# Moving a group norm's load, statistics and coefficients from attention to the end of the layer before

## The chip, the cores and the metric

The kernel runs on one core of a Trainium2 chip. The metric is the device time of one execution in microseconds (us). Each time below is either that of whole executions, measured without a profile, or comes from the one profiled execution; the text says which.

## The reference, cut to what matters

The input x has 8 batch elements of 512 channels by 32 x 32 positions (1024 positions), all in float32. Two layers run one after the other on each element, and no element needs another one.

```python
# layer 0: group norm, attention with 8 heads, output projection, group norm, residual
hn  = group_norm(x, gn1_scale, gn1_bias)          # 32 groups, statistics over 16 channels x 1024 positions
qkv = einsum('bchw,oc->bohw', hn, w_qkv) + b_qkv  # 8 heads of 64 channels
wgt = softmax(einsum('bct,bcs->bts', q * s, k * s))
a   = einsum('bts,bcs->bct', wgt, v)
x   = x + group_norm(einsum('bchw,oc->bohw', a, w_proj) + b_proj, gn2_scale, gn2_bias)

# layer 1: normalised weights, one head over 512 channels, residual
qkv = einsum('oc,bcn->bon', w_qkv1, x);  qkv = qkv / rms(qkv)
attn = softmax(einsum('bci,bcj->bij', q, k) * 512 ** -0.5)
h   = einsum('oc,bcn->bon', w_out, einsum('bij,bcj->bci', attn, v))
x   = (x + h) * 2 ** -0.5
```

## The kernel before

The kernel works through the elements b = 0 to 7 in a Python loop that is fully unrolled (line 1012). Nearly every instruction goes through `InOrder` (line 26), which pins each engine's instructions to the order in which the program names them. So the text of the program is the schedule: each engine (TensorE is PE, VectorE is DVE or `VE`, ScalarE is ACT or `AC`, GpSimd is POOL or `PO`) works through its own list in order, and SyncE's queue (SP, `SY`) issues the transfers in order. Since every instruction passes through that helper, the profile puts nearly all of them on one line, L34; tiles tell them apart.

**Attention (layer 0).** For each element there are 32 steps (`STEPS`), four pairs of heads by eight blocks of 128 rows. `Heads.step(i, fill, early, later)` (line 490) does this in order: `softmax(i)` (two maxima on DVE, two exponentials on ACT, tiles `nm` and `p`); in odd steps from 5 on `values` (16 calls of a matmul, tile `po`, input `pT`); the `fill` list, which holds TensorE work; `scores(i + 1)` (tile `s`, two score tiles of 128 x 1024); `turn()`, which transposes the probabilities of the step before on DVE (tile `pb`) and sends them to `pT` with four transfers; the `early` list; `scale()` (reciprocal on DVE, two multiplies on POOL); and the `later` list. In even steps the `fill` list holds a part of `project_rows` (tile `pqk`), the query and key projection of the next pair of heads; in odd steps it is empty but for what is said of layer 1 below.

Score tiles come from `ps_s`, which has three buffers, and every `scores` takes two of them. Tiles `po`, `pqk`, `pm` and `pv` come from `ps_m` (`bank`), which has two buffers. Large tiles in SBUF come from seven slots (`Slots`, line 37), which are taken and given back by name in program order.

**Norm 1.** `Norm1` (line 300) belongs to the group norm ahead of attention. It loads nothing itself: `load_x` (line 150) brings a quarter of an element (512 KB) into the tile `hn`. `stats` is one `bn_stats` on DVE for half a quarter, eight in all; `aggregate` is four `bn_aggr` (tile `mv`). `GroupNorm.all_steps` (line 291) then averages over each group with a tiny matmul (tile `pm`, which reads `mv`), computes the variance's input with four small DVE operations (tile `d`), does a second tiny matmul (tile `pv`, which reads `d`), and computes the coefficients with seventeen small DVE operations. `apply` multiplies and adds a quarter in place on POOL. Element b + 1 is treated within the attention of element b: the loads stand in steps 4 to 7, the statistics in steps 6 to 13, the aggregate and the pm matmul in step 14, the rest of the coefficients in steps 15 to 21, and the four multiplies in steps 21 and 22.

**Layer 1.** `Layer1.project` (line 724 on) ends with matmuls into the tiles `e`, the unnormalised weights of the second attention, and gives back the slot of the tile `u`, which those matmuls read. What is left is eight products, for two halves `th` of the positions and four quarters `c` of the channels. Here a product is named po(th, c):

```python
def products(self, th, c):     # 8 matmuls 128x512 into a bank, tile po
def keep(self, th, c):         # DVE: multiply po by 1/sum, then add to the residual x
```

`total(th)` is one matmul (tile `pe`) and a DVE reciprocal of the sums, of 128 x 512 elements. `keep` with `th` = 1 also issues the store of its quarter.

The first four products follow one another. The other four are handed on as `fills` and `laters` to steps 0 to 3 of the next element's attention: step c does po(1, c) ahead of `scores(c + 1)`, and keep(1, c) at its end. After step 3 the slots of the element before are given back (`done`).

Of the kernel before, what the change touches and what calls it, by code (L numbers as in the profile page):

```python
# [52 lines left out]
def attention_blocks_kernel(  # L53
# [26 lines left out]
    B, C, H, W = x.shape  # L80
    N = H * W
    NH, D, GROUPS = 8, C // 8, 32
    CI, NT, HN = C // P, N // P, N // 2
# [20 lines left out]
    PE, VE, AC, PO, SY = (InOrder(tc, e) for e in (nc.tensor, nc.vector, nc.scalar, nc.gpsimd, nc.sync))  # L104

    def big(name, lead=CI):

        return slots.take([P, lead, CI * N // lead], name)
# [14 lines left out]
    def run(pieces):  # L123
        for _ in pieces:
            pass
# [4 lines left out]
    x0 = big("hn_0")  # L130
# [19 lines left out]
    def load_x(b, xt, ci):  # L150
        SY.dma_start(out=xt[:, ci, :], in_=xv[b, :, ci, :])
# [82 lines left out]
    def fetch(name, b):  # L234
        SY.dma_start(out=place(name, b), in_=far[name])
# [102 lines left out]
    def project_qk(b, j, hn):  # L338

        qk = pair.tile([P, 2, N], F32, tag="qk", name=f"qk_{b}_{j}")  # L340
        kp = qk[:, 1, :].rearrange("p (be m) -> p be m", be=4)

        def pieces():
            for t in (1, 0):
                w = near["qk"][:, t]
                for th in range(2):
                    hs = slice(th * HN, (th + 1) * HN)
                    pm = bank(f"pqk_{b}_{j}_{t}_{th}")
                    run(matmuls(pm, [(w[:, ci, j * P : (j + 1) * P], hn[:, ci, hs]) for ci in range(CI)]))
                    if t == 0:  # L350
                        AC.activation(qk[:, 0, hs], pm, AF.Identity, bias=bqs[:, j : j + 1], scale=QSCALE0)
                    else:
                        AC.activation(
                            kp[:, :, th * P : (th + 1) * P],
                            pm.rearrange("p (m be) -> p be m", be=4),
                            AF.Identity,
                            bias=col(BK, j),
                        )
                    yield

        return qk, pieces()

    def project_rows(b, j, hn):

        qk = pair.tile([P, 2, N], F32, tag="qk", name=f"qk_{b}_{j}")
        kp = qk[:, 1, :].rearrange("p (be m) -> p be m", be=4)
        spare = near["v#"]

        def pieces():
            for t in (1, 0):
                w = near["qk"][:, t]
                scale = 1.0 if t else QSCALE0
                bias = col(BK, j) if t else bqs[:, j : j + 1]
                for th in range(2):
                    hs = slice(th * HN, (th + 1) * HN)
                    pms = [bank(f"pqk_{b}_{j}_{t}_{th}_{r}") for r in range(2)]
                    for ci in range(CI):
                        for r in range(2):  # L380
                            PE.matmul(
                                pms[r],
                                w[halves[r], ci, j * P : (j + 1) * P],
                                hn[halves[r], ci, hs],
                                start=(ci == 0),
                                stop=(ci == CI - 1),
                            )
                    to, rest = qk[:, 0, hs], spare[:, hs]
                    if t:

                        to = kp[:, :, th * P : (th + 1) * P]
                        rest = rest.rearrange("p (be m) -> p be m", be=4)
                        pms = [pm.rearrange("p (m be) -> p be m", be=4) for pm in pms]
                    AC.activation(to, pms[0], AF.Identity, bias=bias, scale=scale)
                    AC.activation(rest, pms[1], AF.Copy, scale=scale)
                    yield lambda to=to, rest=rest: PO.tensor_add(to, to, rest)

        return qk, pieces()
# [545 lines left out]
    norm1 = Norm1(0, x0)  # L944
# [6 lines left out]
    coeffs = norm1.gn.all_steps()  # L951
# [39 lines left out]
    v0_0 = big("v0_0", NT)  # L991
# [6 lines left out]
    qk0, todo = project_qk(0, 0, x0)  # L998
# [6 lines left out]
        slots.give(name)  # L1005


    heads = Heads(0, x0, v0_0, qk0)
    fills = [[lambda: next(v0)] for _ in range(CI)]
    laters = [[] for _ in range(CI)]  # L1010
    heads.scores(0)
    for b in range(B):
        hn, more = heads.hn, b + 1 < B
        todo = iter(())
        for i in range(STEPS):
            j, r = divmod(i, NB)
            due = []
            fill = [lambda: due.append(next(todo, None))] if (i - LAG) % RG else []
            early, later = [], []
            if i < CI:  # L1020
                fill, later = fills[i] + fill, laters[i]
            if r == 0:
                if j + 1 < CI:
                    heads.qk[j + 1], todo = project_rows(b, j + 1, hn)
                elif more:
                    qk_next, todo = project_rows(b + 1, 0, hn_next)
                if j + 1 == CI:
                    slots.give(f"hn_{b}")
                    if not more:
                        o_last = big(f"o_{b}")  # L1030
                        todo = project_out_half(b, heads, o_last)
            later.append(lambda: [f() for f in due if f])

            if more:


                if i == CI:
                    hn_next = big(f"hn_{b + 1}")
                    norm1 = Norm1(b + 1, hn_next)
                if 0 <= i - CI < CI:  # L1040
                    later.append(lambda: load_x(b + 1, hn_next, i - CI))
                if 0 <= i - CI - 2 < 2 * CI:
                    later.append(lambda: norm1.stats((i - CI - 2) // 2, i % 2))
                k = i - 3 * CI - 2
                if k == 0:
                    coeffs = norm1.gn.all_steps()
                    early += [norm1.aggregate, lambda: next(coeffs)]
                elif 0 < k < 8:
                    early.append(lambda: next(coeffs, None))
                if 0 <= k - 7 < CI // 2:  # L1050
                    for ci in range(2):
                        later.append(lambda ci=ci: norm1.apply(2 * (k - 7) + ci, PO))

            if i == STEPS - NB + 1:
                xt = big(f"x_{b}")
            if 0 <= i - (STEPS - NB + 1) < CI:
                later.append(lambda: load_x(b, xt, i - (STEPS - NB + 1)))
            heads.step(i, fill, early, later)

        if more:  # L1060
            v0_next = big(f"v0_{b + 1}", NT)
            v0 = project_v0(b + 1, hn_next, v0_next)
            next(v0)
        heads.values(STEPS // RG - 2)
        heads.turn()
        if more:
            fetch("proj7", b)
            ta = big(f"ta_{b}").rearrange("p (k i) (h n) -> p k i h n", k=2, h=2)
            rhs = RightSide(heads.a, ta[:, 0], ta[:, 1])
            for j in range(CI // 2 + 1):  # L1070
                rhs.sums(j)
            for _ in range(3):
                next(v0)
        else:
            fetch("score", b)
            begun = OutBegun(b, heads)
        heads.values(STEPS // RG - 1)
        slots.give(f"v0_{b}")
        if more:
            finish_layer0(b, heads, rhs, xt, v0)  # L1080
        else:
            finish_last(b, heads, xt, o_last, begun)
        fetch("value", b)
        one = Layer1(b, xt)
        one.project()
        for c in range(CI):
            one.products(0, c)
            if c == 0:
                one.total(0)
            one.keep(0, c)  # L1090
            if c == 1:
                one.total(1)
        slots.give(f"e_{b}_0")
        if more:
            heads = Heads(b + 1, hn_next, v0_next, qk_next)
            heads.scores(0)
            fills = [[lambda c=c: one.products(1, c)] for c in range(CI)]
            laters = [[lambda c=c: one.keep(1, c)] for c in range(CI)]

            def done(b=b):  # L1100
                for name in (f"v1_{b}", f"e_{b}_1", f"x_{b}"):
                    slots.give(name)

            laters[CI - 1].append(done)
        else:
            for c in range(CI):
                one.products(1, c)
                one.keep(1, c)
# [33 lines left out]
```

## Time and profile before

| what | value |
|---|---|
| runs of the kernel | 3293.03, 3295.05, 3295.7 us; median 3295.05 |
| profiled execution | 3295.35 us, of which the span from the first to the last instruction is 3293.2 |
| PE, DVE, ACT, POOL busy | 99%, 64%, 33%, 30% of the span |
| one `bn_stats` on `hn` (128 x 512) | 0.67 us, 64 of them |
| reciprocal of a sum in layer 1 (128 x 512) | 3.35 us |
| `apply` of a quarter on POOL | 1.19 us |
| one transfer of a quarter into `hn` | 6.1 us from issue to landing |

The busy share says how much of the span an engine spent in instructions. An engine's row in a list of waits says who released it, how long it waited in total, how often, and the longest time. The chain of waits is followed back from the last instruction to whatever released each step, so a hole in TensorE appears there as another engine's piece. A timeline line has the start, the length, the engine, the operation, the tiles (written tile, arrow, tiles read), the shapes, a count, and in brackets the idle time before it with its releaser.

### The profile page before, as it was taken

To read this page: it belongs to the slowest core of one execution; us is meant where nothing else is said; L and a number is where in the kernel's file an instruction comes from. 1 tells how busy PE (TensorE), PEld (TensorE's weight loads), DVE (VectorE), ACT (ScalarE), POOL (GpSimd) and SP (SyncE) were. 2 spreads that over 40 slices of the span, in tenths; PEclk is the share of its full clock that TensorE was granted. 3 is DMA by queue.
4 is the path that set the end of the run, shared out by engine and by line. 5 is a ranking of instruction groups with operands and counts; after the bars stand their busy time and mean duration, and the time that the engine had idled before them with its cause. 6 is when DMAs were issued, how large, how long until landed. Compare 5 with 4: busy or idle time off the path is not lost.

```text
span 3293.2 us, 35605 instructions
## 1 busy us (share of the span) xinstructions
PE 3263.8 (99%) x13178; PEld 1606.6 (49%) x13178; DVE 2118.5 (64%) x2869; ACT 1071.5 (33%) x1813; POOL 983.4 (30%) x857
## 2 busy tenths in 40 slices
PE   8999999999999999999999999999999999999899
PEld 4444544545444454444544445444554545444354
DVE  4696647955488554885449754596645966468653
ACT  2453124521145211551215412254123531145210
POOL 0352123511245022460214503254122531235121
PEclk9999999999999999999999999999999999999899
DMA  5675206741078411782118811287204762057500
GB/s 189 195 196 166 81 6 179 202 150 67 8 205 212 128 45 35 209 219 91 45 53 216 233 52 44 81 219 208 77 13 125 207 177 90 13 140 196 183 7 26
DMA packets 182707, 410.82 MB, mean 125 GB/s; under 512 B 27620, under 2 KB 27656, under 8 KB 176520
## 3 DMA queue, kind: packets, MB, share of 16 engines
q1 hardware_dynamic: 182416, 408.53, 43.6%
q8 instruction: 105, 1.72, 0.2%
q14 instruction: 66, 0.54, 0.0%
q10 hardware_dynamic: 120, 0.02, 0.0%
HBM read 112.48 MB, written 27.56 MB: 43 GB/s over the span
## 4 chain that ended last, share of the span: by engine, by line
PE 94%; DVE 2%; DMA 2%; SPq 1%; issue 1%; DVEq 0%; ACTq 0%
PE po L34 26%; PE s L34 13%; PE pqk L34 12%; PE pv L34 7%; PE p_e_T L34 7%; PE p_e_B L34 5%; PE py L34 4%; PE p_u_T L34 3%; PE p_v_T L34 3%; PE p_o_T L34 3%; PE p_v_B L34 3%; PE p_u_B L34 3%; PE p_o_B L34 2%; DMA pT<-pb 1%; DVE pb L34 1%; PE pG L34 1%
## 5 line engine op out<-in xcount | busy, mean ns | idle before, releaser
L34 POOL TENSOR_SCALAR p<-p,tt 128x1024 f32<-128x1024 f32 x512 | 566.8, 1120 | 917.0 <-DVE tt L34 915.3
L34 ACT ACTIVATE p<-s,nm 128x1024 f32<-128x1024 f32 x512 | 565.9, 1110 | 839.6 <-DVE nm L34 801.1
L34 DVE TENSOR_REDUCE nm<-s 128x1 f32<-128x1024 f32 x512 | 602.1, 1217 | 180.1 <-PE s L34 179.2
L34 DVE STREAM_TRANSPOSE pb<-p 128x2048 f32<-128x2048 f32 x256 | 589.5, 2303 | 29.6 <-POOL p L34 18.8
L34 PE MATMUL s<-qk 64*128 64x512 f32 x2048 | 508.7, 602 | 0.0
L34 PE MATMUL po<-pT,v 128*64 128x256 f32 x4096 | 471.8, 383 | 3.8 <-DMA pT<-pb 2.8
L34 PE MATMUL pqk<-hn,qk 64*128 64x512 f32 (+1 forms) x2016 | 473.9, 591 | 0.0
L34 PE MATMUL po<-e,v 128*128 128x512 f32 x1024 | 450.9, 595 | 0.0
L34 PEld LDWEIGHTS po<-pT,v 128*64 128x64 f32 x4096 | 287.2, 137 | 217.1 <-ACT v L34 68.2
L34 PEld LDWEIGHTS pqk<-hn,qk 64*128 64x128 f32 (+1 forms) x2016 | 201.8, 187 | 252.1 <-issue 240.2
L34 PEld LDWEIGHTS po<-e,v 128*128 128x128 f32 x1024 | 192.2, 190 | 252.7 <-issue 245.5
L34 PEld LDWEIGHTS s<-qk 64*128 64x128 f32 x2048 | 194.4, 186 | 238.8 <-issue 234.2
L34 POOL TENSOR_TENSOR u<-u,xy 128x512 f32<-128x512 f32 x64 | 78.9, 1270 | 762.8 <-DMA xy<-far_rinv 390.2
L34 PE MATMUL pv<-v,hn 128*128 128x512 f32 x512 | 229.0, 598 | 0.0
L34 DVE TENSOR_TENSOR e<-e,p_e_T 128x512 f32<-128x512 f32 x160 | 107.0, 685 | 145.0 <-PE p_e_T L34 142.8
L34 POOL TENSOR_TENSOR qk<-qk,v 128x512 f32<-128x512 f32 x124 | 158.6, 1279 | 83.9 <-ACT v L34 83.9
L34 ACT ACTIVATE e<-e,shift,rinv 128x512 f32<-128x512 f32 x128 | 100.8, 811 | 247.7 <-DVE e L34 247.7
L34 POOL TENSOR_TENSOR esum<-esum,e 128x512 f32<-128x512 f32 x96 | 121.5, 1267 | 163.9 <-ACT e L34 161.4
L34 PEld LDWEIGHTS pv<-v,hn 128*128 128x128 f32 x512 | 94.6, 190 | 115.1 <-issue 114.8
L34 PE MATMUL p_e_T<-s,t 128*128 128x512 f32 x320 | 147.8, 592 | 0.0
L34 PE MATMUL py<-x,gram 128*128 128x512 f32 x320 | 141.6, 602 | 6.0 <-issue 6.0
L34 DVE TENSOR_TENSOR v<-po,esum 128x512 f32<-128x512 f32 x56 | 38.7, 691 | 160.0 <-PE po L34 159.8
(186 smaller groups left out, 3062.3 us busy)
## 6 DMA issues: line engine op xcount, KB each, us to landing
pT<-pb SPq DMA_DIRECT2D x1024, 256.0 KB, 4.4
hn<-in_x_dram SPq DMA_DIRECT2D x32, 512.0 KB, 6.1
x<-in_x_dram SPq DMA_DIRECT2D x32, 512.0 KB, 6.1
out_dram<-x SPq DMA_DIRECT2D x32, 512.0 KB, 3.3
score<-far_score SPq DMA_DIRECT2D x8, 1792.0 KB, 7.6
value<-far_value SPq DMA_DIRECT2D x8, 1792.0 KB, 7.0
qk<-far_qk SPq DMA_DIRECT2D x7, 2048.0 KB, 8.0
proj<-far_proj SPq DMA_DIRECT2D x7, 1792.0 KB, 9.1
```

Of the source, the lines that this page charges most:

```text
L34: return lambda *args, **kw: self._pin(call(*args, **kw))
```

## The change

The norm of element b + 2 is begun at the end of layer 1 of element b. Its tile `hn` is taken there and its four loads are issued ahead of the first product. Six statistics stand behind keep(0, 1) and keep(0, 2), and the last two behind keep(0, 3). The aggregate and the pm matmul come next. Product po(1, 0) and its keep follow outside attention, then the pv matmul and the coefficients, and only then the first scores of the next attention. The other three products stand in steps 0 to 2 of attention, and step 3 has none. The four multiplies stand in steps 1, 3, 5 and 7 of the next element's attention. Element 1 is still treated within the attention of element 0, as before, since nothing comes ahead of it; elements 2 to 7 are treated in the new place.

```diff
@@ steps of attention
-            if more:
+            if b and more and i % 2 and i < 2 * CI:
+                later.append(lambda: norm1.apply(i // 2, PO))
+            if not b:
                 if i == CI:
                     hn_next = big(f"hn_{b + 1}")
                     norm1 = Norm1(b + 1, hn_next)
...
@@ end of layer 1
         one = Layer1(b, xt)
         one.project()
+        hn_now = hn_next
+        if b + 2 < B:
+            hn_next = big(f"hn_{b + 2}")
+            norm1 = Norm1(b + 2, hn_next)
+            for c in range(CI):
+                load_x(b + 2, hn_next, c)
         for c in range(CI):
             one.products(0, c)
             if c == 0:
                 one.total(0)
             one.keep(0, c)
             if c == 1:
                 one.total(1)
+            if c and b + 2 < B:
+                for ci in (0, 1) if c == 1 else (c,):
+                    for k in range(2):
+                        norm1.stats(ci, k)
         slots.give(f"e_{b}_0")
         if more:
-            heads = Heads(b + 1, hn_next, v0_next, qk_next)
+            if b + 2 < B:
+                norm1.aggregate()
+                coeffs = norm1.gn.all_steps()
+                next(coeffs)
+                next(coeffs)
+            one.products(1, 0)
+            one.keep(1, 0)
+            if b + 2 < B:
+                run(coeffs)
+            heads = Heads(b + 1, hn_now, v0_next, qk_next)
             heads.scores(0)
-            fills = [[lambda c=c: one.products(1, c)] for c in range(CI)]
-            laters = [[lambda c=c: one.keep(1, c)] for c in range(CI)]
+            fills = [[lambda c=c: one.products(1, c)] for c in range(1, CI)] + [[]]
+            laters = [[lambda c=c: one.keep(1, c)] for c in range(1, CI)] + [[]]
...
-            laters[CI - 1].append(done)
+            laters[CI - 2].append(done)
```

## Prediction

> **What bounds the kernel now.** I read the page first, then TensorE's own waits, then the chain of waits around the passage from one element to the next, then the timeline of the same stretch. In the page's busy line TensorE (PE) is at 99%, every other engine at 64% or less:
>
> ```profile
> PE 3263.8 (99%) x13178; PEld 1606.6 (49%) x13178; DVE 2118.5 (64%) x2869; ACT 1071.5 (33%) x1813; POOL 983.4 (30%) x857
> ```
>
> So only what TensorE waits for, or what it executes, counts. Its waits, from the list of who waited for whom:
>
> ```profile
> PE py L34 <- issue: 6.0, 1, 6.0
> ...
> PE pm L34 <- DVE mv L34: 4.0, 1, 4.0
> PE po L34 <- DMA pT<-pb: 2.8, 1, 2.8
> ```
>
> Each of these three happened once, all in the last element, which computes no norm1. The attention that holds norm1 today shows no waiting: the windows view gives 42.69 us of busy PE in 42.69 us for 1338.72 to 1381.41, eight steps with statistics in them, 10.67 us a pair of steps, the pace of a pair without them (1403.49 to 1414.16 in the chain). At 64% VectorE (DVE) is not the bound, and freeing it gives TensorE nothing there.
>
> The chain of waits over one passage (element 2 to 3) gives the order that the change alters:
>
> ```profile
> 1269.83 13.73 PE po L34 x32
> 1283.57 1.92 PE s L34 x8
> 1285.48 7.06 PE po L34 x16
> 1292.55 4.05 PE pqk L34 x15
> ...
> 1319.27 1.72 PE s L34 x7
> 1320.99 7.06 PE po L34 x16
> 1328.05 1.92 PE s L34 x8
> 1329.97 3.43 PE pqk L34 x16
> ```
>
> po x16 is one `products` call, s x8 one `scores`. See that a product stands between every two score groups up to step 3, and that PE has no hole. A score group costs 1.92 after a product and 1.72 after pqk; a product 7.06 after scores and 6.87 (half of 13.73) after a product. Each change of shape thus costs 0.2.
>
> What step 3's product hides is in the timeline: scores 3 end at 1320.99, but the first exponential, which frees a score tile, ends at 1322.61:
>
> ```profile
> 1320.18 2.36 DVE L34 TENSOR_REDUCE nm<-s 128x1 f32<-128x1024 f32 x2 [3.94 <-PE s L34]
> ...
> 1321.50 1.11 ACT L34 ACTIVATE p<-s,nm 128x1024 f32<-128x1024 f32 x1 [1.60 <-DVE nm L34]
> ```
>
> The last element shows the chain that the change puts behind `keep(0, 3)`, with TensorE idle in front of it:
>
> ```profile
> 3103.57 1.29 DVE L34 BATCH_NORM_STATS2 st<-o 128x6 f32<-128x512 f32 x2
> 3104.89 0.21 DVE L34 BATCH_NORM_AGGREGATE mv<-st 128x2 f32<-128x12 f32 x1
> 3105.15 0.51 PE L34 MATMUL pm<-mv,gavg 128*128 128x4 f32 x2 [3.95 <-DVE mv L34]
> ```
>
> And the windows view shows what a 2.83 us hole (3075.46 to 3078.29) did to the clock (last columns: granted clock, DMA share, GB/s):
>
> ```profile
> 3078.00:3084.00 6.00, 5.71 (x34) 3.55 (x35) 2.31 (x1) 0.47 (x1) 0.81 (x1) 0.72 0.85 212
> ```
>
> **What the Trainium skill says.** "TensorE: Matmul & The Clock Gate", Part 1, says that TensorE falls to half clock after an idle window of about 3.4 us and needs a busy window of that length to recover; the window runs freely. This trace agrees on the price and is harsher on the threshold: after 2.83 us the 32 po matmuls took 5.18 instead of 3.67, and the clock of 0.72 over 6 us is 3.4 us at half speed, so 1.7 us lost. The same page, Part 3 ("What overlaps and what doesn't"), says that matmuls start and end in program order; the pm above, waiting with everything behind it, agrees. "PSUM — Partial Sum Buffer", Engine vs sequencer instructions, says that VectorE's queue is strict FIFO; the timeline shows nothing else.
>
> **The change part by part.** In the built program PE's order is po(0,3), pm, po(1,0), pv, scores 0; DVE's is keep(0,3), two statistics, four aggregates, four small operations for the mean, keep(1,0), seventeen small operations, first maximum.
>
> *1. A new wait at pm, 6 passages (b = 0 to 5).* pm needs the aggregate, which stands behind keep(0,3), which needs po(0,3) whole. The DVE chain from the end of po(0,3): keep 1.45 (1283.57 to 1285.02: two of 0.69 with gaps), two statistics 1.31, four aggregates 0.38 (attention's row of four), hand-over 0.04: 3.2 us of idle TensorE. Queued behind pm: po(1,0), scores 0, everything. pm itself 0.15 (its pair is 0.32 in today's chain, shape change included; ends 0.05 and 0.5). 6 x 3.35 = +20.1. pv follows po(1,0) by which time d is long ready: 6 x 0.15 = +0.9.
>
> *2. The clock after it.* 3.2 us is longer than the hole that cost 1.7. As the window runs freely I take 70% of six: +7.1; ends 0 and 18.6 (3.1 each, what py lost after the last element's long hole: 20.30 against 17.17).
>
> *3. Step 3 loses its product, 7 passages (b = 0 to 6).* po(1,0) leaves step 0, the others move up one step, step 3's list is empty. Scores 4 follow scores 3 at once, with three score tiles of which they need two: the first is free, the second is the one that exponential 3 frees 1.62 after scores 3. Scores 4 then need two more passes of 0.43, so they end 2.55 after scores 3 instead of 1.72: +0.85. Behind it DVE (maximum, transpose 2.30, maximum) and ACT run late: exponential 4 ends when pqk ends (+0.1), and the drain of pqk, behind exponential 4's second half, holds the bank that values(0) needs (+0.5). By step 6 they have caught up, since a step asks 4.8 us of DVE (2.35 + 2.30 + 0.13) against 5.34 of PE. 7 x 1.45 = +10.2; ends 0.8 and 3.0 each (a whole maximum and exponential, plus a late bank).
>
> *4. Shape changes.* Scores 4 after scores 3 save 0.20, po(1,0) after a 128-row matmul 0.19: 7 x 0.39 = -2.7.
>
> *5. pm and pv leave attention, 6 elements.* In today's chain the pair of steps with pm lasts 11.10 (1381.41 to 1392.51), that with pv 10.98, against 10.67: 6 x (0.43 + 0.31) = -4.4.
>
> *6. Priced at nothing.* Eight statistics (0.67) and the small operations leave attention: no PE wait there today. Six of the statistics run in the 3.0 us hole after the second reciprocal (1270.35, 3.35 long) and in the 5.5 us hole before keep(0,3); four of them end at about 1276.3, keep(0,2) is due at 1276.74. If that cover goes, keep(0,3)'s chain lengthens. The seventeen operations (3.35, timeline of the last element, 3107.13 to 3110.46) put the first maximum 4.8 us after po(1,0); po(1,1) and pqk, 11 us, hide it, and keep(1,1)'s multiply, next on DVE, has 0.4 to spare before pqk wants its bank. Four loads on SP move from steps 4 to 7 to the release of u at 1254.4: SP has only stores behind them, the DMA share there is 0.00, a 2048 KB fetch lands in 8.0, issue takes up to 1.8 each, so all are in by about 1267; DVE asks at 1273.7. On POOL four multiplies of 1.19 move to steps 1, 3, 5, 7, each ahead of the next `scale`, where POOL idles 3 us and more. Slots: hn takes u's place; the pT tiles of steps 1 to 5 get slots whose last readers end about 10 us before or earlier.
>
> **Sum:** 20.1 + 0.9 + 7.1 + 10.2 - 2.7 - 4.4 = +31.2. The profiled execution took 3295.35 (span 3293.2 and 2.15 around it), 0.3 above the median of the runs: 3326.
>
> **Rivals.**
> *A: the clock holds.* The hole stays under the gate's window, pm costs 3.35 only: 3295 + 24 = 3319. For: 3.2 is under the skill's 3.4. Against: 2.83 sufficed once. 14%.
> *B: step 3 runs DVE into arrears.* Transposes then also wait for the pT transfers, of which 1 MB leaves per step (one waited 0.69 at 1343.72): 3.5 us a passage instead of 1.45: 3340. 11%.
> *C, not slower: no hole at pm.* If the statistics of the last quarter and the aggregate were done before po(0,3) ends, pm would find its operand ready. Place: DVE's queue in those 6.87 us, idle for 4 of them. Price: -20.1 - 7.1. It decides from the point where the last statistics stand ahead of keep(0,3). Then 3299, within no change; if exponential 3 is hidden too, 3289. The built order, keep first, speaks against it. 4%.
> *D: the loads come late,* DVE stands in front of keep(0,2) and pm waits 3 us longer: 3345 or more. Seven us of margin say no. 3%.
>
> **How the numbers follow.** The likeliest case, 68%, gives 3326. The range 3309 to 3343 holds A and B, and the ends of 2 and 3 except where both lie at an end together; C and most of D are left out. A measurement tells about 0.2% (6.6 us) from no change: faster 0.02 and same 0.03 are C with and without the exponential, and 0.01 for an error in the sum; slower 0.95.
>
> **What would show it.** TensorE's waits after: "pm from DVE mv" six more times, near 3.2 each; a clock below 1.00 in the windows behind some of them; score groups 3 and 4 adjacent with a hole near 1.2 and a values group half a us late; no pm or pv inside attention from element 1 on. Wrong, if pm's wait is absent or under 2 us, if holes over 3 us appear in step 3, or if DVE waits for hn.

## The result, and the profile after

The changed kernel takes 3330.64 us (median of 6 runs, 3326.19 to 3342.92) against 3295.7 us (median of 6, 3293.03 to 3298.18): a ratio of 1.0111, 95% interval 1.0092 to 1.0131. It is slower by about 1.1%, at 3330.64 against the predicted 3326. Its runs scatter over 17 us, those of before over 5. The profiled execution of the changed kernel took 3334.11 (span 3332.2, which is 39.0 more than before).

TensorE's share fell to 98% while its instruction count stayed the same:

```profile
PE 3272.9 (98%) x13178; PEld 1607.6 (48%) x13178; DVE 2127.5 (64%) x2869; ACT 1073.0 (32%) x1813; POOL 982.7 (29%) x857
```

Who TensorE waited for (total us, times, longest):

```profile
PE pm L34 <- DVE mv L34: 22.1, 7, 4.0
PE s L34 <- ACT p L34: 12.4, 7, 1.8
PE py L34 <- issue: 6.0, 1, 6.0
...
PE po L34 <- DMA pT<-pb: 2.9, 1, 2.9
```

Two rows differ from before. The pm row had one entry of 4.0, in the last element; it now has seven, so the six new ones are 18.1 us, 3.0 each. The wait of the scores for an exponential did not exist; it comes seven times, once per passage (the stretch from one element's layer 1 to the next one's attention), 1.8 each.

The chain of waits over the passage from element 2 to 3 shows both places, each time as pieces of other engines between pieces of PE:

```profile
1285.38 13.75 PE po L34 x32
1299.13 0.02 issue
1299.15 0.70 DVE v L34
1299.85 0.02 issue
1299.88 0.69 DVE x L34
1300.57 1.20 DVE st L34 x2
1301.76 0.34 DVE mv L34 x4
1302.10 0.04 issue
1302.14 0.59 PE pm L34 x2
1302.73 9.64 PE po L34 x16
1312.37 0.12 PE pv L34 x2
1312.49 1.92 PE s L34 x8
...
1348.19 0.89 PE s L34 x5
1349.09 0.02 issue
1349.11 1.24 DVE nm L34
1350.34 0.02 issue
1350.37 0.02 ACTq L34
1350.38 0.04 issue
1350.43 1.21 ACT p L34 x2
1351.64 0.04 issue
1351.68 1.55 PE s L34 x5
```

The upper part is keep(0, 3) (v, then x), the last two statistics (st), the four aggregates (mv), then pm: 3.03 us without TensorE. Then po(1, 0), an ordinary product of 6.87, takes 9.64. The lower part is step 3: maximum 3, exponential 3, and only then scores 4.

What happened to po(1, 0) is in the windows view of this passage and the next one, in which the hole was as long (columns: window, length, five engines, granted clock, DMA share, GB/s):

```profile
1302.70:1312.40 9.70, 9.70 (x19) 4.21 (x18) 0.65 (x4) 0.00 (x0) 0.00 (x0) 0.73 0.00 0
1708.80:1715.80 7.00, 7.00 (x19) 3.17 (x18) 0.64 (x4) 0.00 (x0) 0.00 (x0) 1.00 0.00 0
```

The clock was 0.73 in one and 1.00 in the other. PE is busy throughout in both, so the busy share hides this loss.

I measure a passage from the start of po(0, 0) to the start of the first `values`, both read off the chain. From element 2 to 3 these are, before and after:

```profile
1254.38 6.87 PE po L34 x16
1335.12 3.60 PE po L34 x32
```

```profile
1269.93 6.87 PE po L34 x16
1358.82 3.60 PE po L34 x32
```

Before, a passage is 80.74 us, and the same wherever the chain shows it whole. After, the seven are 88.91, 88.90, 88.89, 86.02, 86.01, 87.71 and 82.38: longer by 8.17, 8.16, 8.15, 5.28, 5.27, 6.97 and 1.64, in sum 43.6. The last one has no norm, and shows step 3 alone: 1.64. Two have norm and full clock: 5.27, of which 3.6 are the hole, pm and pv. The other four lost 2.9, 2.9, 2.9 and 1.7 more, which is the clock, 10.4 in all. Attention between the passages (from the first `values` to the next po(0, 0)) was 318.04 to 318.69 in the six elements 1 to 6 and is 317.31 to 317.39: a gain of 5.7. With 0.8 and 0.2 us lost at the start and in the last element, the sum is 43.6 - 5.7 + 1.0 = 38.9 of the 39.0.

### The profile page after: what moved, and what is told of

It reads as the page before. It is cut to its first block, busy times and chain, and to the rows that moved or that the text cites. A ratio compares the mean times of both kernels' runs of the same rounds, so it can differ in the third digit from the quotient of the medians.

```text
span 3332.2 us, 35659 instructions
## 1 busy us (share of the span) xinstructions
PE 3272.9 (98%) x13178; PEld 1607.6 (48%) x13178; DVE 2127.5 (64%) x2869; ACT 1073.0 (32%) x1813; POOL 982.7 (29%) x857
## 3 DMA queue, kind: packets, MB, share of 16 engines
q8 instruction: 105, 1.72, 0.2%
## 4 chain that ended last, share of the span: by engine, by line
PE 98%; DVE 1%; issue 0%; ACT 0%; DMA 0%; SPq 0%; ACTq 0%; DVEq 0%
PE po L34 27%; PE s L34 14%; PE pqk L34 14%; PE pv L34 7%; PE p_e_T L34 7%; PE p_e_B L34 5%; PE py L34 4%; PE p_u_T L34 3%; PE p_v_T L34 3%; PE p_o_T L34 3%; PE p_v_B L34 2%; PE p_u_B L34 2%; PE p_o_B L34 2%; PE pG L34 1%; PE pA L34 0%; PE pB L34 0%
## 5 line engine op out<-in xcount | busy, mean ns | idle before, releaser
L34 PE MATMUL po<-e,v 128*128 128x512 f32 x1024 | 460.2, 605 | 0.0
```

The source lines that it names most:

```text
L34: return lambda *args, **kw: self._pin(call(*args, **kw))
```

## The experiments

**e1_hole_gone: order on VectorE alone.** The loads and all DVE work of the norm stay at the end of layer 1.

```diff
         for c in range(CI):
             one.products(0, c)
...
+            if c == CI - 1 and b + 2 < B:
+                for k in range(2):
+                    norm1.stats(c, k)
+                norm1.aggregate()
             one.keep(0, c)
...
-            if c and b + 2 < B:
+            if 0 < c < CI - 1 and b + 2 < B:
...
-                norm1.aggregate()
                 coeffs = norm1.gn.all_steps()
```

> The last two statistics and the aggregate stand ahead of keep(0,3) on VectorE instead of behind it; everything else is as in the changed kernel. Theory (the time went into the hole at pm, the slower clock after it, and step 3): the six holes of 3.03 us and every loss of clock vanish, pm costs some 0.15 us instead of 0.39, step 3 keeps its 1.8 us wait: 3304 us, 9 above the kernel before. Rival (the moved loads and statistics crowd the end of layer 1, whatever their order): 3325 to 3335 as in the changed kernel, with the lost time at other waits.

Measured: 3307.88 (ratio to before 1.004, interval 1.0025 to 1.0055), 23 us less than the changed kernel, with runs from 3306.53 to 3309.47. The chain of the same passage:

```profile
1273.81 13.75 PE po L34 x32
1287.56 0.02 issue
1287.58 0.70 DVE v L34
1288.28 0.04 issue
1288.33 7.13 PE po L34 x16
```

The hole at pm is gone and po(1, 0) runs at full pace. The rival that the moved work crowds the end of layer 1, whatever its order, falls: the same work in the same place, in another order on one engine, costs 23 us less. The forecast of 3304 missed 4 us, and the list of waits names them, a wait that the hole had covered:

```profile
PE po L34 <- DVE v L34: 4.0, 6, 0.7
```

There are two banks (buffers for the results of matmuls): pm has taken the one that po(0, 2) left, so po(1, 0) needs that of po(0, 3) and waits for the first half of keep(0, 3), 0.7 us, six times.

**e2_hole_half and e3_hole_long: the length of the hole.** In e2 only the statistics move ahead of keep(0, 3). In e3 the changed kernel gets four more statistics in front of the aggregate:

```diff
+                for k in (0, 1, 0, 1):
+                    norm1.stats(CI - 1, k)
                 norm1.aggregate()
```

> Only the last two statistics move ahead of keep(0,3); the aggregate stays behind it. Theory: the hole shrinks from 3.03 to 1.8 us, and with so short a hole the clock stays at 1.00: 3317 us, with runs close together. If the clock is lost after any hole at all: up to 10 us more, 3327. Rival of crowding: no change from the changed kernel.

> Four statistics are added ahead of the aggregate (the last quarter's two, twice over; the result is the same), so that the hole grows from 3.03 to about 5.6 us. Theory: with a hole longer than any window of the gate, every one of the six passages loses the clock, 2.9 us each as in the worst passages of the changed kernel, in every run: 3324 + 15.7 + 17.4 = 3357 us, and the runs scatter less than those of the changed kernel (3326 to 3343). If the loss were a matter of chance for every length, about 3346 with the same scatter.

Measured: e2 3320.27 (3318.28 to 3322.25; ratio 1.0077, interval 1.0062 to 1.0092), e3 3351.57 (3351.07 to 3352.97; ratio 1.0173, interval 1.0156 to 1.019). The hole of e2 is 1.83 us. My expectation that so short a hole leaves the clock alone was wrong: in three passages it does, in the other three it doesn't. Two neighbouring passages of e2, from the chain:

```profile
489.40 0.39 PE pm L34 x2
489.78 8.67 PE po L34 x16
```

```profile
893.23 0.39 PE pm L34 x2
893.62 6.97 PE po L34 x16
```

The product loses 1.70 us or nothing, never a part. In e3, with a hole of 5.4 us instead of the 5.6 expected, every passage loses: po(1, 0) takes 8.39 to 9.61, and pm 0.59 instead of 0.39. That is 2.2 us a passage on average, where I had written 2.9; with the hole 0.2 shorter, it is why e3 came out 5 us under its forecast. As expected, the runs lie within 2 us of one another, where those of the changed kernel lie within 17.

What decides is when the hole begins. The Trainium skill ("TensorE: Matmul & The Clock Gate", Part 1) states a free-running window of 3413 ns. The trace records the granted clock itself, and it agrees. In the changed kernel the clock falls to 0.50 in four passages, at 488.77, 894.96, 1301.15 and 2516.29, which lie 119, 119 and 356 times 3.4133 us apart; it stays there for two windows (6.83) in the first three and for one (3.41) in the fourth. The windows view around the third fall, and around the first one of e2, with the clock as the third figure from the end:

```profile
1297.74:1301.15 3.41, 1.37 (x4) 0.30 (x2) 1.96 (x4) 0.00 (x0) 0.00 (x0) 1.00 0.01 2
1301.15:1307.98 6.83, 5.84 (x9) 2.74 (x10) 1.59 (x10) 0.00 (x0) 0.00 (x0) 0.50 0.00 0
1307.98:1311.39 3.41, 3.41 (x10) 1.50 (x9) 0.00 (x0) 0.00 (x0) 0.00 (x0) 1.00 0.00 0
```

```profile
486.91:490.32 3.41, 1.56 (x6) 0.68 (x5) 2.15 (x9) 0.00 (x0) 0.00 (x0) 1.00 0.00 0
490.32:493.73 3.41, 3.41 (x5) 1.37 (x5) 0.22 (x2) 0.00 (x0) 0.00 (x0) 0.50 0.00 0
493.73:497.14 3.41, 3.41 (x9) 1.47 (x9) 0.00 (x0) 0.00 (x0) 0.00 (x0) 1.00 0.00 0
```

These instants give the boundaries of the windows in each execution. The next table puts the start of each hole (start of pm less the length of the hole) after the last boundary; e5, described below, has the hole of the changed kernel:

| hole | us from the boundary to the start of the hole, and length of po(1,0) there |
|---|---|
| 1.83 us (e2) | 0.66, 0.87, 1.08: 8.67; 1.51, 1.72, 2.15: 6.97 |
| 3.03 us (changed kernel and e5) | 1.08: 9.80; 1.34, 1.37, 1.40: 9.66, 9.65, 9.64; 1.49, 1.78, 1.89, 2.05: 6.97; 2.52, 2.59, 2.86, 3.33: 8.67 |
| 5.4 us (e3) | 1.20, 1.43, 1.54: 8.56, 8.44, 8.39; 2.49, 2.67, 2.72: 9.61, 9.52, 9.50 |

The places sort the losses of all 24 holes without an exception. The loss is half of what is left of the slow stretch when the hole ends: in the third passage of the changed kernel, the stretch runs for 6.83 and the hole covers its first 0.99, which gives 2.9; a hole that is over before the clock falls costs half a window, 1.70. In e3 the loss therefore falls by half a us for each us that the hole begins later, within each group. The traces do not agree with the skill's advice to avoid idle gaps over about 3 us (same page, "Why this matters for your kernels"): 1.83 us is enough where it falls badly. How much idle time in a window it takes stays open. All of the 1.83 us lay in one window when the hole began at 0.66, and cost 1.70; all of it lay in one window as well when it began at 1.51, and cost nothing.

**e4_product_moved: step 3 alone.** The kernel before, with the norm where it was:

```diff
         if more:
+            one.products(1, 0)
+            one.keep(1, 0)
             heads = Heads(b + 1, hn_next, v0_next, qk_next)
             heads.scores(0)
-            fills = [[lambda c=c: one.products(1, c)] for c in range(CI)]
-            laters = [[lambda c=c: one.keep(1, c)] for c in range(CI)]
+            fills = [[lambda c=c: one.products(1, c)] for c in range(1, CI)] + [[]]
+            laters = [[lambda c=c: one.keep(1, c)] for c in range(1, CI)] + [[]]
```

> The kernel before with one part of the change only: po(1,0) stands ahead of scores 0 and step 3 has no product; the group norm stays within attention. Theory: each of seven passages loses 1.64 us net (2.04 of waiting at scores 4 less 0.39 of shape changes): 3295.4 + 11.5 = 3307 us, no hole at pm, clock 1.00. Rival (step 3 costs only since the norm's multiplies and coefficients stand near it): under 3299 us.

Measured: 3306.8 (3306.5 to 3308.45; ratio 1.0037, interval 1.0024 to 1.005), 11.9 above the 3294.86 of the kernel before, measured beside it, for 11.5 expected. Its list of waits has the same row as the changed kernel:

```profile
PE s L34 <- ACT p L34: 12.4, 7, 1.8
```

So step 3 costs this with or without the norm beside it.

**e5_step3_filled: something else in step 3.** The changed kernel, with pqk moved one step:

```diff
-            fill = [lambda: due.append(next(todo, None))] if (i - LAG) % RG else []
+            fill = [lambda: due.append(next(todo, None))] if (i in (0, 3) if b and i < CI else (i - LAG) % RG) else []
```

> The changed kernel with one pqk part moved from step 2 to step 3 in elements 1 to 7; a product cannot stand in step 3, since the seven slots are all taken there (hn of the element after the next holds one, and pT of step 3 needs the one that v1 gives back). Theory: the 3.43 us of pqk cover exponential 3, so the seven waits of 1.8 us at scores 4 vanish (2.04 us a passage), and pqk no longer waits for a bank behind a product in step 2 (some 0.85 us a passage); the hole at pm and its clock stay: 3330.6 - 20 = 3310 us. Rival (the lost time at step 3 is VectorE in arrears, which would only come out elsewhere): above 3320.

Measured: 3310.44 (3307.05 to 3311.99; ratio 1.0042, interval 1.0026 to 1.0057), the 3310 that was expected. No wait of the scores is left, and the holes at pm stay as they were (22.1 us in seven waits). The last passage, which has no norm, falls from 82.38 to 79.50: 2.04 are the wait at scores 4, and 0.84 are what pqk no longer loses behind a product in step 2. Step 3's loss was a missing cover, not VectorE in arrears.

**e6_both_mended and e7_two_ahead: the terms together.** e6 has the edits of e1 and e5, and pm and pv of this norm in a score tile (`norm1.gn.bank` replaces `bank` there). e7 adds:

```diff
             if b + 2 < B:
                 run(coeffs)
+            one.products(1, 1)
+            one.keep(1, 1)
...
-            fills = [[lambda c=c: one.products(1, c)] for c in range(1, CI)] + [[]]
+            fills = [[], [lambda: one.products(1, 2)], [lambda: one.products(1, 3)], []]
```

> Statistics and aggregate ahead of keep(0,3), as in e1_hole_gone; pm and pv of this norm in a score tile instead of a bank, so that po(1,0) needn't wait 0.66 us for keep(0,3) as it did there; and pqk in step 3, as in e5_step3_filled. Theory: the three terms add, so with all of them gone: 3307.9 - 4.0 - 20.2 = 3284 us, 0.34% below the kernel before, and no wait of TensorE at a passage. If the terms overlap: above 3290.

> As e6_both_mended, and po(1,1) too stands ahead of scores 0, so that step 0 has pqk alone: another 1.24 us for each of seven passages (one change of shape, and pqk's wait for a bank behind a product): 3275 us. If maximum and exponential 0 come late behind the coefficients, up to 2 us a passage are given back: 3285 to 3290.

Measured: e6 3283.02 (ratio 0.9962, interval 0.9949 to 0.9974), e7 3275.1 (ratio 0.9937, interval 0.9925 to 0.995), both within 1 us of the forecast. The terms add up, and both kernels beat the kernel before and the changed one. The chain of e7 at the passage has nothing but PE in it:

```profile
1277.96 0.12 PE pm L34 x2
1278.08 6.97 PE po L34 x16
1285.05 0.12 PE pv L34 x2
1285.17 6.97 PE po L34 x16
1292.14 1.92 PE s L34 x8
1294.06 3.43 PE pqk L34 x16
1297.49 1.72 PE s L34 x8
```

A pm that finds its operand ready costs 0.12. The pqk in step 0, with no product in front of it, takes 3.43 and the scores behind it 1.72, where the two took 6.20 before (1292.55 to 1298.75 in the kernel before): the product ahead of it had cost 1.05 more, a change of shape and a wait for its bank.

**e8_norm_stays: the same products, the old norm.** The kernel before, with po(1, 0) and po(1, 1) ahead of scores 0 and the other two products in steps 1 and 3.

> The kernel before, the norm within attention, but po(1,0) and po(1,1) ahead of scores 0 and the other two products in steps 1 and 3. Theory: 2 x 1.24 us for each of seven passages: 3294.9 - 17.4 = 3277.5 us. Against e7_two_ahead this tells what the moved norm alone is worth once its waits are mended: about 2.5 us, of the 5.7 us that attention gained less what pm and pv cost in the new place. If e7 is not faster than this one, moving the norm brings nothing.

Measured: 3278.47 (3276.96 to 3280.47; ratio 0.9949, interval 0.9937 to 0.9962). Most of e7's gain is thus the place of the products and not the norm. Moving the norm, once nothing waits for it, is worth 3.4 us (3278.47 - 3275.1; the ranges of the runs don't overlap), for 2.5 expected. In the two profiled executions, 3.1 apart, six elements gain 0.74 each in attention (318.05 to 317.31) and lose 0.44 each in the passage (78.25 to 78.69), 1.8 in sum; 0.8 more is one wait at pm in e8.

## Why the prediction was right, point by point

The direction, the size and both places were right. By its steps, with the profiled execution beside them:

1. *The wait at pm:* 20.1 foretold and 0.9 for pv. Measured 6 x (3.03 + 0.39) = 20.5 and 6 x 0.12 = 0.7. The aggregates and statistics were slightly shorter (0.34 and 1.20), pm after a hole longer (0.39 to 0.59). e1 shows the cause.
2. *The clock:* 7.1 foretold, 10.4 measured in this execution. The step took one loss of 1.7 in 70% of passages; three of six lost 2.9, one 1.7, two nothing. The share was about right and the price too low, because the clock can stay down for two windows. Even the hole that the price was taken from lost 1.5 and not 1.7 (5.18 against 3.67): it ended 0.3 after the clock fell. Without its 10.4 this execution would have taken 3323.7. The six runs lie 2.5 to 19.2 above that, 6.9 in the median; this is an estimate of their clock losses, which puts all of their scatter down to the clock. So it is in part luck that 7.1 fits the median run: where a hole falls in the window changes from run to run.
3. *Step 3:* 10.2 foretold (1.45 a passage). Measured 2.04, the net 1.64 and the 0.39 of shape changes together: 14.3 over seven. The mis-sized part is scores 4 in the wait. I let both rows of the first score tile run while the second was awaited; but `scores` alternates between its two tiles, and the trace shows a wait of 1.77 with all but the first of eight passes behind it. The lateness that I placed at the following steps (0.5 for a bank) didn't come: after scores 4 nothing waits. e4 and e5 show the cause.
4. *Shape changes:* -2.7, not measured apart; the 1.64 of the last passage fits it, and e4 with it.
5. *pm and pv out of attention:* -4.4 foretold, -5.7 measured. They account for 0.74 an element, as foretold: e1, with the norm outside, takes 317.30 from values to po(0, 0), and e4, with the norm inside, 318.05. The rest is 0.1 to 0.6 in five elements of the kernel before only, where VectorE's transposes waited for the pT transfers more often (8.4 us in 11 waits, and 3.3 in 7 after):

```profile
2557.26 2.31 DVE L34 STREAM_TRANSPOSE pb<-p 128x2048 f32<-128x2048 f32 x1 [1.37 <-DMA pT<-pb]
```

That line is of the kernel before, in a step that loads hn. Since e4 loads hn in the same steps and shows no such loss, the load alone isn't the cause; this part, 1.3 us in all, stays open.

6. *Priced at nothing:* right. No wait for a transfer into hn appears on VectorE, and the four issues took 1.76 us from 1270.07, right behind the release of u. The coefficients in front of the first maximum cost nothing.

Foretold was +31.2. By the medians of the runs it is +34.9, and the 3.7 between them are in the main step 3 (4.1). By the span of the profiled execution it is +39.0, with 3.3 more from step 2, since this execution lost more clock than the median one. Of the rivals, A (the clock holds) happened in two of six passages, where a boundary divided the hole and neither window had more than 1.92 us of it. C (nothing behind keep) was built as e1 and came to 3307.88, not 3299. Its sum left out the wait for the bank (4.0), and it inherited step 3's error (4.1). B and D didn't happen.

## What to carry to other kernels

On an engine at 99%, a moved step costs nothing only if its result is ready before the busy engine's queue reaches the instruction that reads it. Look at what stands ahead of the producer on its own queue: here the order of two items on VectorE was worth 23 us. When work is taken out of a step to make room elsewhere, ask what that work covered there: step 3's product covered an exponential, and 3.43 us of another matmul did as well (e5).

## What was not expected of the hardware

A hole of 1.83 us in TensorE's work cost 1.70 us of clock in half of the cases, depending on where it fell in a window of 3.41 us (e2), and one of 0.7 us (e1) cost none in six. Holes of 3.03 us cost 0 to 3.0 (changed kernel and e5), and holes of 5.4 us cost 1.6 to 2.8 (e3). A hole of 3.03 us that began 1.40 us into a window cost 2.9, and one that began at 1.49 nothing. What was lost is shown as busy time of TensorE; only the granted clock tells it.
